# Layer 1's 3x3 convolutions in groups of four columns from six terms, and attention's order taken from a table

## The chip, the cores and the metric

The kernel runs on one core of one Trainium2 chip. The metric is device time in microseconds of one execution. Before the change it is 1324.69 us, the median of three runs (1323.67 to 1330.67). The profile comes from one more execution of its own.

## What is computed

The input x is 16 images of 128 channels and 32x32 pixels, all in float32. Two "metaformer" layers are applied, each with a mixer and a feed-forward part and with residual additions:

```
# layer 0
x = x + attention(ln_c(x))              # linear attention, 4 heads
t = tokens(x)                           # 1024 tokens x 128 channels for each image
t = t + stu(ln_t(t))                    # spectral convolution over the tokens + 3 taps
# layer 1
x = x + conv_block(ln_c(x))             # two 3x3 convolutions
t = tokens(x)
t = t + experts(ln_t(t))                # 64 experts, each takes its 8 best tokens
```

The convolution block is what the change rewrites first:

```
out = relu(bn(conv3x3(x, w1), gamma1, beta1, mean1, var1))
out = bn(conv3x3(out, w2), gamma2, beta2, mean2, var2)
return relu(out + x)                    # x is the normalized image here
```

## The kernel before, in words

The program runs stage after stage: **attention** (with the forward transform and the three taps of layer 0's feed-forward part) for 16 samples, **generation** (the spectral product, 16 chunks), **layer 1** for 16 samples (inverse transform, convolutions, routing, gates, pooling), the **experts** (16 groups of four, whose weights stream from memory), and a **final** addition and store. Inside a stage the samples overlap, and each engine works through its instructions in the order in which the program lists them (`tc.manual_schedule` pins PE, DVE, ACT and POOL). So the order of the list decides who waits for whom.

*Attention.* Class `Attention` has one method for each step of a sample. The order is a hand-written tuple `period` of 61 entries (name, distance): a loop over p from -6 to 15 runs each entry for sample p + distance, so seven samples are in flight and one sample is finished in each round. Work for later stages is cut in pieces and run between the entries: `filters()` builds the spectra of the filters and the mixed matrices `mst` (its 16 pieces `mi` are loaded and added on DVE, L662 to L667), and `prepare()` on POOL turns the 3x3 weights into the terms `cwd` (L678 to L694) and scales the inverse transform (L699 to L706). One piece of each runs in a round.

*Layer 1.* Class `Routed` has one method for each step of a sample. The order comes from `table`: each row has a name, an engine, a duration, a due time, the steps that it waits for and the buffers that it opens and closes. `planned()` (L1475) is a list scheduler that runs when the program is built: it takes, among the steps that can start within 0.25 us of the earliest one, the one with the smallest due time (offset + b x 54.66), with 0.15 us for a hop from engine to engine. A buffer that opens takes the slot that is free first.

*The convolutions.* A row of 32 columns is cut into 16 pairs. Two output columns come from four terms: the input terms are d0-d2, d1+d2, d2-d1 and d1-d3 of four neighbouring columns (`terms`, L914, on DVE, one instruction of 544 elements per partition for each term, from the padded planes `pads`); each term is multiplied by its own weights and summed over the three rows dy on PE (`products`, L922); and the two columns come back from sums and differences. An image is done in two halves of 16 rows. For one half of one convolution:

- `middle` (PE): terms 1 and 2, 2 x 3 products of 256 columns (L926) into one PSUM bank `pcv`, of which there are three;
- `shift` (ACT, L1097) copies one product out of PSUM; `sums` (DVE, L1105 and L1106) makes sum and difference;
- `outer` (PE): terms 0 and 3, again 2 x 3 products (L926);
- `rows` (DVE, L1115 and L1116) adds them; `relu` (ACT, L1119) writes the first convolution's result into the padded planes; `rows2` adds the residual (L1143) and the sample itself (L1145).

So one sample has 2 convolutions x 2 halves x 12 = 48 products of 256 columns. In the trace each float32 product is two records (2 x 16 x 48 = 1536). The other PE steps of a sample are `inverse` (L1039), transposes (L149, L159), `logits` (L1187), `turn` (L149) and `pool` (L1242); the last three run once for two samples. Of the buffers, the term tile `v` and the result tile `r` have two slots each, the PSUM tile `big` two, the token tile `tok` one.

*Loads.* SP issues nearly all transfers in its own queue. Layer 1 first loads `wi`, `cw`, the gate weights and `b1` (L890 to L901), then for each sample x and y (L942, L945). The experts' weights go through a ring of nine 1 MB slots (`RING`) made of tiles that layer 1 no longer needs: five slots are loaded after the last sample's `inverse`, four after its last `rows2`.

Of the kernel before, what the change touches and what calls it, by code (L numbers as in the profile page):

```python
# [1 line left out]

# [12 lines left out]
P = 128  # L15
# [15 lines left out]
NQ = 8  # L31
# [26 lines left out]
HP = H + 2  # L58
WP = W // 2 + 1
HR = H // 2  # L60
WT = W // 2
# [5 lines left out]
def metaformer_kernel(ctx: ExitStack, tc: tile.TileContext, io: dict, out: bass.AP):  # L67
# [96 lines left out]
    with ExitStack() as l0:  # L164
# [7 lines left out]
        cwd = [dram.tile([P, 3, 4, C], F32, name=f"cwd{n}", tag=f"cwd{n}") for n in range(2)]  # L172
# [32 lines left out]
        ph = lconst.tile([P, NCH, CW], F32, name="ph")  # L205


        with ExitStack() as a0:
# [96 lines left out]
            for b in range(2):  # L305
                load(b)
            wqk = aconst.tile([P, 2 * C], F32, name="wqk")
# [16 lines left out]
            nc.vector.tensor_scalar(mu[:, 0], mu[:, 0], wmix[:, 0:1], None, ALU.mult)  # L324
            for i in range(1, NF):
                nc.vector.scalar_tensor_tensor(
                    mu[:, i], mu[:, i], wmix[:, i : i + 1], mu[:, i - 1], ALU.mult, ALU.add
                )

# [11 lines left out]
            class Attention:  # L341
# [10 lines left out]
                def tokens(self):  # L352
                    if self.b + 2 < B:
                        load(self.b + 2)
# [37 lines left out]
                def norm(self):  # L392
                    normalize(self.tok, self.tok, self.sts[:, 0], self.sts[:, 3])
# [19 lines left out]
                def q_(self):  # L413
# [17 lines left out]
                def k(self):  # L431
# [69 lines left out]
                def fold2(self):  # L501
# [4 lines left out]
                def fold2_copy(self):  # L506
                    self.wt = work.tile([P, P], F32, name="wt", tag="wt")
                    nc.vector.tensor_copy(self.wt, self.pw)
# [37 lines left out]
                def norm2(self):  # L546
                    normalize(self.ub, self.ub, self.sts2[:, 0], self.sts2[:, 3])
# [64 lines left out]
                def taps(self):  # L612

                    self.pa = big()
                    for si, (lo, hi) in enumerate(SEGS):
                        for tap in range(KU):
                            a = max(lo, tap)
                            nc.tensor.matmul(  # L618
                                self.pa[:, a:hi], mu[:, NF - 1 - si, tap, :],
                                self.u[:, a - tap : hi - tap],  # L620
                                start=(tap == 0), stop=(tap == KU - 1),
                            )
# [5 lines left out]
            def filters():  # L628

                wfm = setup.tile([P, NQ // 2, 2 * P], F32, name="wfm", tag="mi")  # L630
# [970 lines left out]
```

## Time and profile before

| what | value |
|---|---|
| median of three runs | 1324.69 us |
| the profiled execution's own time | 1324.0 us |
| its span, first to last instruction | 1322.2 us |
| around the span | 1.8 us |
| mean granted TensorE clock | 0.971 |
| attention, 0 to 395 us | PE busy 54.65 of the first 80 us, 304.72 of the other 315 |
| generation, 395 to 681 us | PE busy 278.42 of 286 |
| layer 1 starts, 681 to 724 us | PE busy 19.81 of 43 |
| layer 1, 724 to 1182 us | PE busy 456.24 of 458 |
| its last serial chain, 1182 to 1217 us | PE busy 22.81 of 35 |
| experts, 1217 to 1290 us | DMA share 0.93 |
| final, 1290 to 1322 us | DMA share 0.64 |

The stage borders were read from the timeline; they are where the first or last instruction of a kind stands. "PE" is the matmul part of TensorE and "PEld" its weight load, which overlaps it. A busy PE says that matmuls were in flight, not that they ran at peak. In a group of instructions the "busy" figure is the union of their times, so that two instructions that overlap count once; the "mean" is that of one record from its start to its end, and for pipelined matmuls it is longer than the distance from one to the next. The chain of waits lists what ended last, step by step, and there the distance can be read.

### The profile page before, as it was taken

Reading aid. Unit: us, or ns where it says so; the run is one execution under the profiler, and the core shown is the slowest. Engines: PE = TensorE matmul, PEld = TensorE weight load, DVE = VectorE, ACT = ScalarE, POOL = GpSimd, SP = SyncE. Lnnn points to the kernel's source line nnn. Section 1 sums busy time; section 2 is a strip of 40 time slices with the busy share of each in tenths; the row PEclk is TensorE's granted clock in tenths of the full one; section 3 lists DMA queues with packets and bytes.
Section 4 is the critical chain, followed back from the end, with each engine's and each line's share of the span. In section 5 each row is a group of like instructions: output and inputs, shape, how many; then the busy total and the mean of one; then the engine's idle time right before and its main releaser. Section 6 shows DMA issues by size and latency. Waiting matters only on the chain. (4 is left out here: it accounts for less than half of the span.)

```text
span 1322.2 us, 33734 instructions
## 1 busy us (share of the span) xinstructions
PE 1216.7 (92%) x14116; PEld 990.8 (75%) x14116; DVE 907.2 (69%) x1982; ACT 705.2 (53%) x1424; POOL 503.3 (38%) x816
## 2 busy tenths in 40 slices
PE   4889999999998999999956999999999999996886
PEld 3777777777767888888846987989888888883443
DVE  5688887877765666776637767777778676772224
ACT  3777777777545666666623435545555454544111
POOL 2324545454685777777743111222212121110002
PEclk8899999999998999999987999999999999997998
DMA  7014343433344333333367211313122113007986
GB/s 268 17 35 140 118 134 112 144 124 121 114 149 145 127 125 127 127 121 119 107 235 182 70 48 49 88 27 111 32 80 64 33 49 127 17 24 260 374 329 255
DMA packets 87401, 162.99 MB, mean 123 GB/s; under 512 B 5584, under 2 KB 40784, under 8 KB 86864
## 3 DMA queue, kind: packets, MB, share of 16 engines
q1 hardware_dynamic: 86608, 158.33, 36.2%
q8 instruction: 111, 1.82, 0.6%
q0 software_dynamic: 640, 2.49, 0.5%
q14 instruction: 42, 0.34, 0.1%
HBM read 104.18 MB, written 56.62 MB: 122 GB/s over the span
## 5 line engine op out<-in xcount | busy, mean ns | idle before, releaser
L926 PE MATMUL pcv<-v,cw 128*128 128x256 f32 x1536 | 342.9, 380 | 0.0
L926 PEld LDWEIGHTS pcv<-v,cw 128*128 128x128 f32 x1536 | 286.8, 190 | 42.2 <-issue 5.7
L785 ACT COPY g<-pg 128x512 f32<-128x512 f32 x288 | 153.1, 591 | 102.8 <-PE pg L776 102.8
L783 DVE COPY g<-pg 128x512 f32<-128x512 f32 x224 | 145.8, 687 | 90.1 <-PE pg L776 90.1
L776 PE MATMUL pg<-ph,mst 32*128 32x128 f32 x4096 | 155.3, 287 | 4.5 <-ACT g L785 3.0
L776 PEld LDWEIGHTS pg<-ph,mst 32*128 32x128 f32 x4096 | 130.7, 190 | 30.8 <-issue 25.9
L796 PE MATMUL py<-g,v 128*32 128x128 f32 x4096 | 140.1, 276 | 3.8 <-POOL v L768 1.2
L796 PEld LDWEIGHTS py<-g,v 128*32 128x32 f32 x4096 | 105.3, 110 | 20.7 <-issue 2.4
L767 POOL TENSOR_TENSOR v<-xc 128x256 f32<-128x256 f32 x128 | 91.6, 741 | 71.6 <-PE py L796 62.5
L141 ACT ACTIVATE tok<-tok,sts 128x128 f32<-128x128 f32 x256 | 101.8, 481 | 23.8 <-POOL sts L1001 20.4
L132 DVE BATCH_NORM_STATS2 bst<-big 128x6 f32<-128x256 f32 x256 | 91.1, 417 | 19.5 <-PE big L154 12.1
L1066 POOL TENSOR_SCALAR sts<-bst 128x8 f32<-128x8 f32 x16 | 6.5, 406 | 235.7 <-DVE bst L132 235.7
L920 DVE TENSOR_TENSOR v<-pads 128x544 f32<-128x544 f32 x128 | 85.0, 723 | 9.9 <-ACT pads L1119 9.5
L618 PE MATMUL big<-u,mu 128*128 128x128 f32 (+4 forms) x384 | 86.0, 380 | 0.0
L274 POOL TENSOR_TENSOR xf<-ab 128x256 f32<-128x256 f32 x34 | 24.8, 730 | 132.0 <-DVE ab L241 131.9
L618 PEld LDWEIGHTS big<-u,mu 128*128 128x128 f32 x384 | 56.7, 191 | 18.0 <-issue 15.4
L1097 ACT ACTIVATE ct<-pcv,bn 128x256 f32<-128x256 f32 x64 | 30.3, 474 | 68.8 <-PE pcv L926 67.9
L551 PE MATMUL big<-wf,ub 128*128 128x256 f32 x256 | 62.0, 385 | 0.2
L149 PEld LDWEIGHTS big<-ident,x 128*128 128x128 f32 x384 | 47.3, 148 | 19.2 <-issue 7.2
L149 PE MATMUL big<-ident,x 128*128 128x128 f32 x384 | 53.6, 286 | 8.5 <-DVE x L1048 3.4
L1115 DVE TENSOR_TENSOR r<-pcv,cs 128x256 f32<-128x256 f32 x64 | 26.9, 420 | 49.0 <-PE pcv L926 48.2
L141 ACT ACTIVATE tt<-tt,sts 128x128 f32<-128x128 f32 x128 | 51.1, 480 | 9.2 <-POOL sts L1001 8.9
(231 smaller groups left out, 2271.3 us busy)
## 6 DMA issues: line engine op xcount, KB each, us to landing
we<-in_weight SPq DMA_DIRECT2D x32, 1024.0 KB, 9.7
vd<-xf SPq DMA_DIRECT2D x16, 1024.0 KB, 5.1
xc<-vd SPq DMA_DIRECT2D x64, 256.0 KB, 3.5
yd<-ys SPq DMA_DIRECT2D x32, 512.0 KB, 3.8
y<-yd SPq DMA_DIRECT2D x15, 896.0 KB, 6.5
x<-in_x SPq DMA_DIRECT2D x16, 512.0 KB, 4.1
mi<-in_M_phi SPq DMA_DIRECT2D x16, 512.0 KB, 4.9
xd<-x SPq DMA_DIRECT2D x16, 512.0 KB, 6.0
```

What stands on the lines that cost most here:

```text
L132: nc.vector.bn_stats(bst[:, j : j + 2, :].rearrange("p j s -> p (j s)"), src[:, j : j + 2, :].rearrange("p j c -> p c j"),)
L141: nc.scalar.activation(dst[:, j, :], src[:, j, :], AF.Identity, bias=nm[:, j : j + 1], scale=r[:, j : j + 1],)
L149: nc.tensor.transpose(pt[:, j, :], src[:, j * P : (j + 1) * P], ident)
L551: nc.tensor.matmul(dst, self.ub[:, q, :], wf[:, q, :], start=True, stop=True)
L618: nc.tensor.matmul(self.pa[:, a:hi], mu[:, NF - 1 - si, tap, :], self.u[:, a - tap : hi - tap], start=(tap == 0), stop=(tap == KU - 1),)
L767: nc.gpsimd.tensor_tensor(vv[:, x, 1:, bs], e, o, op)
L776: nc.tensor.matmul(pg[r][:, i], mst[rs, 4 * q + i, :], ph[rs, c, :], start=True, stop=True,)
L783: nc.vector.tensor_copy(dst, src)
L785: nc.scalar.copy(dst, src)
L796: nc.tensor.matmul(py[rows, x, kl, :], v[:, (x * NM + m) * JL + jl, 1 - ri : 3 - ri, :] .rearrange("p k b -> p (k b)"), g[:, ((x * 2 + ri) ...
L920: nc.vector.tensor_tensor(v[:, k], d[i], d[j], op)
L926: nc.tensor.matmul(pc[:, i], wt[:, dy, k, :], v[:, k, hf * HR + dy : hf * HR + dy + HR], start=(dy == 0), stop=(dy == 2),)
```

## The change

Three parts, in one diff.

**1. Four columns from six terms.** A row is cut into 8 groups of four columns. Four output columns come from six terms, so one convolution of a whole image is 6 x 3 products of 8 x 32 = 256 columns; the upper and lower rows are no longer padded, and the products of dy = 0 and 2 leave one row out (248 columns). The halves are gone: a product fills a bank for the whole image.

```
-        def products(v, wt, hf, ks):
-            pc = ps.tile([P, 2, HR, WT], F32, name="pcv", tag="cv", bufs=3)
+        def products(v, wt, ks):
+            pc = ps.tile([P, 2, IMG], F32, name="pcv", tag="cv", bufs=3)
             for i, k in enumerate(ks):
-                for dy in range(3):
+                for dy in (1, 0, 2):
+                    lo, hi = max(0, 1 - dy), min(H, H + 1 - dy)
                     nc.tensor.matmul(
-                        pc[:, i], wt[:, dy, k, :], v[:, k, hf * HR + dy : hf * HR + dy + HR],
-                        start=(dy == 0), stop=(dy == 2),
+                        pc[:, i, lo * GT : hi * GT], wt[:, dy, k, :],
+                        v[:, k, lo + dy - 1 : hi + dy - 1],
+                        start=(dy == 1), stop=(dy == 2),
                     )
```

The first convolution's terms are no longer made on DVE: PE multiplies the normalized tokens by a constant matrix `bt` (a new input), 8 products of 192 columns, and ACT copies them out of PSUM. The image itself is still transposed and copied, for the residual.

```
+            def terms(self, i):
+                pv = self.pv[i] = big().rearrange("p (j w) -> p j w", j=4)
+                for j in range(4):
+                    nc.tensor.matmul(
+                        pv[:, j, : NTERM * 4 * GT], self.tok[:, 4 * i + j], bt, start=True, stop=True
+                    )
+            def terms_copy(self, i):
+                rows = slice(i * H // 2, (i + 1) * H // 2)
+                nc.scalar.copy(
+                    va[:, :, rows].rearrange("p t (j r) g -> p t j (r g)", j=4),
+                    self.pv[i][:, :, : NTERM * 4 * GT].rearrange("p j (t w) -> p t j w", t=NTERM),
+                )
```

The second convolution's terms are made on DVE, from padded planes of 32 x 9 = 288 elements; two planes at once are 576 elements (`columns(i, k)` addresses column sets i and k).

```
+            def inside_terms(self):
+                v = self.v = vb
+                zt = self.zt = work.tile([P, 4, PLANE], F32, name="zt", tag="zt", bufs=1)
+                nc.vector.scalar_tensor_tensor(
+                    zt[:, 0:2], columns(2, 1), -4.0, columns(4, 3), ALU.mult, ALU.add
+                )
+                nc.vector.tensor_tensor(v[:, 1], zt[:, 0], zt[:, 1], ALU.add)
+                nc.vector.tensor_tensor(v[:, 2], zt[:, 0], zt[:, 1], ALU.subtract)
+            def next_terms(self):
+                v, zt = self.v, self.zt
+                nc.vector.tensor_tensor(zt[:, 2:4], columns(4, 3), columns(2, 1), ALU.subtract)
+                for k, f in ((3, 2.0), (4, -2.0)):
+                    nc.vector.scalar_tensor_tensor(
+                        v[:, k], zt[:, 3], f, zt[:, 2], ALU.mult, ALU.add
+                    )
+            def outer_terms(self):
+                v05 = self.v[:, 0::5]
+                nc.vector.scalar_tensor_tensor(
+                    v05, columns(0, 1), 4.0, columns(4, 5), ALU.mult, ALU.add
+                )
+                nc.vector.scalar_tensor_tensor(v05, columns(2, 3), -5.0, v05, ALU.mult, ALU.add)
```

The output columns come from three pairs of products, `inside` (terms 1, 2), `next` (3, 4) and `outer` (0, 5). ACT copies the second product of the first two pairs (256 elements each); the rest is on DVE. The shift of the first batch normalization moves into the relu's bias, that of the second into `rest`.

```
+            def inside_sums(self):
+                sd = self.sd = work.tile([P, 2, IMG], F32, name="cs", tag="cs")
+                m = self.pc[1, 2][:, 0]
+                nc.vector.tensor_tensor(sd[:, 0], m, self.cti, ALU.add)
+                nc.vector.tensor_tensor(sd[:, 1], m, self.cti, ALU.subtract)
+            def columns(self):
+                nd = work.tile([P, 2, IMG], F32, name="zt", tag="zt", bufs=1)
+                m = self.pc[3, 4][:, 0]
+                nc.vector.scalar_tensor_tensor(nd[:, 0], self.ctn, 0.5, m, ALU.mult, ALU.add)
+                nc.vector.scalar_tensor_tensor(nd[:, 1], m, 2.0, self.ctn, ALU.mult, ALU.subtract)
+                r = self.r = work.tile([P, 4, IMG], F32, name="r", tag="r", bufs=1)
+                nc.vector.tensor_tensor(r[:, 0:2], nd, self.sd, ALU.add)
+                nc.vector.scalar_tensor_tensor(r[:, 2:4], nd, 4.0, self.sd, ALU.mult, ALU.add)
+            def edges(self):
+                y03 = self.r[:, 0::3]
+                nc.vector.tensor_tensor(y03, self.pc[0, 5], y03, ALU.add)
...
+            def rest(self):
+                self.edges()
+                r = self.r
                 nc.vector.scalar_tensor_tensor(
+                    r, r, bn[:, 1, 1:2], self.p1.rearrange("p o h k -> p o (h k)"), ALU.add, ALU.add
+                )
+                xs = self.x.rearrange("p (n o) -> p n o", o=4)
+                nc.vector.scalar_tensor_tensor(
+                    xs, r.rearrange("p o n -> p n o"), 0.0, xs, ALU.max, ALU.add
                 )
```

The tiles `va` (first convolution), `vb` (second), `r` and `zt` have one slot each, `zt` now being shared by the inverse transform's odd classes, `columns` and the second convolution's terms. The weights grow from 4 to 6 terms (`cwd`, two loads of 1152 KB in place of 768 KB), and `prepare()` needs more steps on POOL for them: after the three scalings, 3 additions of 384 elements, a scaling of 768, then scaling, addition, scaling, 2 additions, a scaling of 768 and one more scaling, in place of 3 additions and a scaling of 768.

**2. Layer 1's table** is rewritten for these steps, with new due times (offset + b x 206.95). `planned()` gets `in_turn=True` here: a buffer takes its slots in rotation. `even` and `odd` are now one after the other, and samples may start at 0, 4, 8 and 12 us of the plan.

**3. Attention's order** comes from `planned()` as well. The tuple `period` is replaced by a table of the same steps with durations, due times (offset + b x 113.05) and buffers; `norm`, `norm2` and `taps` are cut in two. The filters are steps of the table (`f_mixes`, `f_negate`, `f_even` and so on). The pieces of `mst` may start at 30 + 10 b us and those of `prepare`, three at a time, at 70 + 17 b us of the plan. At the start x0, x1, `wf`, `phi` and x2 to x7 are loaded in this order, before the first 3x3 weights.

```
-                for p in range(-reach, B):
-                    next(preparing, None)
-                    for name, d in period:
-                        b = p + d
...
+            def ready(b, name):
+                if name == "tokens":
+                    return 2.0 * b if b < 2 else 8.5 + 1.5 * b
+                if name == "f_matrix":
+                    return 30.0 + 10.0 * b
+                if name == "prepare":
+                    return 70.0 + 17.0 * b
+                return inputs.get(name, 0.0)
+            inputs = dict(f_mixes=6.5, f_negate=6.0, f_even=9.5, f_odd=9.5)
...
+                for b, name in planned(
+                    table, buffers, B, 113.05, left_out, ready
+                ):
```

Around them: `b1` is loaded into `tok`'s slot after the last `image`; the ring's order is y, z, wi, y, cw0, v, cw1, zt, pad, with four slots loaded after the last `inverse`, one after the last `outer_a`, four after the last `rest`; the experts' outputs `ot` lie in `lg`'s slot and the gates of pair 4 in `tok`'s; the final stage's copy `yt` takes the slots of the weights.

## The prediction

> **What bounds the kernel now.** I read the busy shares first, then busy time by stage, then the chain of waits inside layer 1, then the rows of the instructions that go. The shares and the chain by line, from the page:
>
> ```profile
> PE 1216.7 (92%) x14116; PEld 990.8 (75%) x14116; DVE 907.2 (69%) x1982; ACT 705.2 (53%) x1424; POOL 503.3 (38%) x816
> ...
> PE pcv L926 25%; PE big L1039 4%; PE big L149 3%; PE big L159 2%; PE big L1187 1%; PE pp L1242 1%; PE peo L1405 1%; DMA we<-in_weight 1%; PE ph L1381 1%; PE pfy L1461 1%; PE ph L1374 1%; DVE ht L1396 1%; DMA y<-yd 1%; PE pht L1394 1%; DMA yd<-ys 0%
> ```
>
> PE is the busy one, and the products of the convolutions (L926) hold a quarter of the path. Shares are averages, so the same by stage (length; then busy time of PE, weight load, DVE, ACT, POOL; clock; DMA):
>
> ```profile
> 0.00:80.00 80.00, 54.65 (x282) 44.62 (x283) 51.45 (x176) 46.78 (x98) 20.95 (x33) 0.89 0.32 118
> 80.00:395.00 315.00, 304.72 (x1771) 237.22 (x1769) 246.98 (x564) 214.92 (x442) 164.19 (x265) 1.00 0.40 125
> ...
> 724.00:1182.00 458.00, 456.24 (x2693) 400.21 (x2692) 345.45 (x745) 230.20 (x464) 89.56 (x222) 1.00 0.20 59
> ...
> 900.00:1021.30 121.30, 121.30 (x740) 106.67 (x738) 94.91 (x206) 63.62 (x129) 25.77 (x64) 1.00 0.22 61
> ```
>
> In layer 1 PE never rests; DVE is idle over a fifth of the time. 121.30 us are four samples (the pooling, L1242, returns each 60.67 us for two), so a sample takes 30.33 us, with 23.7 of DVE and 15.9 of ACT. Attention is nearly as full after 80 us; its first 80 us leave PE 25 us idle. The chain of waits inside layer 1 gives distances, cleaner than means:
>
> ```profile
> 904.36 1.90 PE pp L1242 x32
> ...
> 920.48 10.36 PE pcv L926 x48
> ...
> 949.36 3.57 PE big L1039 x32
> ...
> 960.70 0.87 PE big L159 x8
> ```
>
> 48 records are 24 products: 0.432 us for 256 columns. Twice 10.36 is a sample's 48 products, 20.72 of its 30.33 us.
>
> **Part 1, PE in layer 1.** Removed: 20.72 us a sample. Added: 36 products, 12 of 256 columns (0.432) and 24 of 248 (0.418 by columns): 5.18 + 10.04 = 15.2. Also added: 8 products of 192 columns, 8 x 0.324 = 2.6, by columns from the same row. Net -2.9 us a sample, -46.6 for sixteen, all on the path while PE sets the pace. By columns is safe down to 128: L1039's sixteen products of 128 take 3.57 us, 0.223 each. If the 192-column products went at the weight load's mean of 190 ns a record, they would cost 3.0: 7 us in all, kept for the range.
>
> **Part 1, DVE.** The rows that go:
>
> ```profile
> L920 DVE TENSOR_TENSOR v<-pads 128x544 f32<-128x544 f32 x128 | 85.0, 723 | 9.9 <-ACT pads L1119 9.5 <-ACT pads L1083 0.4
> ...
> L1115 DVE TENSOR_TENSOR r<-pcv,cs 128x256 f32<-128x256 f32 x64 | 26.9, 420 | 49.0 <-PE pcv L926 48.2
> ...
> L1097 ACT ACTIVATE ct<-pcv,bn 128x256 f32<-128x256 f32 x64 | 30.3, 474 | 68.8 <-PE pcv L926 67.9
> ```
>
> Busy by count: a term 85.0 / 128 = 0.664; 256 elements 0.42; 512 elements (L1143) 0.69; 1024 (L1048) 1.22. Removed a sample: 8 terms 5.3, 16 instructions of 256 (sums and rows) 6.6, L1143 and L1145 twice 2.8: 14.7. Added, scaled between these rows (288: 0.45, 576: 0.70): inside sums 4 x 0.42 = 1.7; `columns` twice (2 x 0.42 + 2 x 0.69) = 4.4; edges 2 x 0.69 = 1.4; second terms 4 x 0.70 + 4 x 0.45 = 4.6; `rest` 2 x 1.22 = 2.4: 14.5. So DVE stays at 23.5 us, but of a 27.4 us sample: 86% in place of 78%. ACT: four shifts (1.9) go, four copies of 256 (0.386, L822: 1.5) and two of 768 (0.8, between L785's 0.59 for 512 and L1063's 1.01 for 1024) come: 15.9 + 1.2 = 17.1 us, 63%. Both remain beside PE's work; the cover is thinner.
>
> **What is late next.** The tile `r` has one slot, and its round for a sample is: columns 2.2, edges 0.7, two relus 1.25 (L1119), inside terms 1.6, two PE groups 5.1, copy 0.4, columns 2.2, rest 3.1, and eight hops of about 0.1: 17.4 us. It fits in 27.4, but 9.9 of it are DVE's, and DVE has 13.6 us of other work to place. Where an instruction of DVE stands in front, the products behind it wait on PE, and PE's queue with them. Two gaps in PE's chain can open: outer_a to inside_b (edges, relus, inside terms, hops: 3.9 us) and after outer_b (`rest` 3.1 us until the next columns may start). Each must be covered by PE's other 12.2 us a sample (inverse, transposes, terms, routing). Bounds: 0 idle (now 1.8 us of 458) to 7.0 a sample. I take 0.6, nearer to today's rows, since the same kind of order holds PE at 99.6% now and DVE still has 4 us a sample free: +10 us. The drain: nothing else covers the last sample's 3.9 us gap, and `rest` (3.1) ends later than the old last half (0.8 + 1.4): +3, bounds 0 to 5. Layer 1: -46.6 + 10 + 3 = **-34**.
>
> **Part 1, the borders of the stage.** Layer 1 starts after yd has been written (6.60 us) and y(1) read (9.03 us, until 702.4): the loads of weights grow by 0.86 MB with `bt` in front of them, issued when the last generation products free their memory at about 663; DMA's share from 660 to 680 is 0.52, so they hide there; uncovered they cost 2 us at the 410 GB/s seen at the start. `even` before `odd` puts 1.5 us of POOL ahead of DVE in the first sample, while `add` no longer stands behind y(1)'s landing (it waited from 701.4 to 705.6): 0, bounds -3 to +2. The ring still has five slots loaded before the last `rest` and four after it; the experts are DMA-bound (0.93) and stay. The gates of pair 4, on SP, now wait for `tok` until the last group has used `b1` and hold back pairs 5 and 6; they are needed last of eight: 0, bounds 0 to 2. `yt` in the weights' slots: 0.
>
> **Part 3, attention.** The taps are PE's last work for a sample, and their distance is the round (start, duration):
>
> ```profile
> 269.94 5.38 PE L618 MATMUL big<-u,mu 128*128 128x128 f32 x24
> ...
> 291.83 5.38 PE L618 MATMUL big<-u,mu 128*128 128x128 f32 x24
> ```
>
> 21.89 us, nine times over. Adding the starts of one round's PE groups where nothing waits gives 20.7; the rest is a wait for the normalized `ub` (L530) at `taps_in` and what follows it. An order that moves these apart can win 1.1; I take 0.6 in 11 rounds: -7. The fill: of 25 us idle in the first 80, 6 pass before the first product (6.18), and phi, behind the same loads as now, lands at 16.6. DVE and ACT are both under 65% there, so earlier samples can start earlier: -10. From 25 to 40 us the clock is at 0.50 to 0.58 with 10.5 us of matmuls; a fuller PE keeps some of the 5 us lost: -2. Attention: **-19**. Bounds: -36 (all of the 1.1 in 14 rounds, 15 of the idle, 5 of clock) to +8 (0.4 of new stalls in 20 rounds).
>
> The preparation adds to POOL, per convolution, from 5.2 us to 13.5 (five steps of 1.0, two scalings of 2.15, three more at half of 2.15), 17 us in all. Behind them on POOL stand `k_scale`, which PE's `context` waits for, and the butterflies. POOL is half idle there (164 of 315): 0; if each of some 16 pieces held PE up by half its 2.4 us, +19, a bound I keep only in part, as DVE's k_recip comes 2 us ahead of it. One row speaks against more POOL work: at 695.29 L966 on DVE takes 0.95 us beside a POOL addition and 0.42 at 702.87 without. [...]
>
> The sum against the profiled execution: 1324.0 - 34 - 19 = 1271, say **1270**. That execution stands 0.7 below the median, so nothing is to be added.
>
> **Rivals.**
> - *Attention's table wins nothing* (the round stays 21.9, the fill is bound by DVE's chain in each sample): 1324 - 34 = 1289. For it: PE is already 97% busy after 80 us.
> - *DVE at 86% shows on PE*: 1.5 us idle a sample, 1324 - 46.6 + 24 + 3 - 19 = 1285. For it: one slot each of `r`, `va`, `vb`, `zt`; against: DVE waits for PE today (L1115, 48 us).
> - *Better*: no new idle time in layer 1, attention near its bound: 1324 - 46.6 - 31 = 1246.
> - *It does not do what it says*: PE time does not follow columns (the 192-column products go at the weight load's 190 ns): 1277.
> - *Slower*: the two PE gaps between convolutions stay open because PE's order has nothing ready to put in. With 5 of the 7.0 us open: 1324 - 46.6 + 80 + 3 - 19 = 1341. It decides from 2.9 + (19 - 3) / 16 = 3.9 us a sample on. Against it: 12.2 us of other PE work a sample, and two samples' tiles alive.
>
> **How the numbers follow.** Chances: forecast 0.46, attention nothing 0.19, DVE 0.15, better 0.11, not by columns 0.03, slower 0.06. Low 1246 takes in the better case as far as its worked value, high 1308 the DVE rival with attention winning nothing (1304) and 4 us of the small bounds. About 0.5% is what a measurement can tell from no change. Faster by more 0.90, within 0.04, slower 0.06.
>
> **What would show it.** Layer 1: pooling every 54.8 to 57 us in place of 60.67, L926 at about 243 us in the chain's distances, PE idle near 10 us, DVE share about 0.85. Attention: taps about 21 us apart, the first of them well before 94.8, generation starting near 376 in place of 395. A PE gap after each `outer_a`, waiting for DVE terms, is the slower rival; waits of L618 or `context` on POOL are the preparation. I am wrong if the products do not shrink with columns, or if PE's idle time in layer 1 passes 3.9 us a sample.

## The result, and the profile after

The changed kernel takes 1331.65 us, the median of 20 runs, against 1324.87 us for 20 runs of the kernel before. The ratio is 1.0061, with a 95% interval of 1.0043 to 1.0079: **slower by 0.6%**. The forecast was 1270 us, faster.

First the shares, the chain that ended last by line, and the costliest group of PE, from the page of the changed kernel. A group's row ends with the idle time of its engine just before it and with what ended that:

```profile
PE 1187.6 (90%) x13988; PEld 962.0 (73%) x13988; DVE 954.5 (72%) x1918; ACT 725.1 (55%) x1456; POOL 509.4 (38%) x830
...
PE pcv L1058 18%; PE big L1222 3%; PE big L1172 2%; PE big L149 2%; PE big L159 2%; PE big L1396 1%; DVE bst L132 1%; DMA we<-in_weight 1%; PE peo L1620 1%; PE ph L1594 1%; PE ph L1587 1%; DVE v L1256 1%; DVE v L1253 1%; PE pfy L1676 1%; DVE ht L1611 1%
...
L1058 PE MATMUL pcv<-v,cw 128*128 128x248 f32 (+1 forms) x1152 | 262.5, 381 | 24.0 <-DVE v L1256 20.6
```

PE has 29 us less to do than before (1187.6 against 1216.7) and the span is 4.4 us longer. The products now stand behind 24.0 us of idle PE, nearly all of it ended by one DVE line, L1256, the second instruction of `outer_terms`; and two DVE lines that write the input terms (L1256 and L1253) have entered the chain. Next the stages of the changed kernel by windows (length; busy time of PE, weight load, DVE, ACT, POOL; clock; DMA):

```profile
0.00:80.00 80.00, 62.27 (x321) 49.03 (x322) 62.99 (x181) 51.13 (x106) 23.61 (x42) 0.89 0.38 139
80.00:395.00 315.00, 299.32 (x1726) 233.25 (x1725) 260.98 (x558) 212.96 (x434) 176.14 (x261) 0.99 0.38 120
...
725.10:1185.80 460.70, 433.94 (x2655) 380.41 (x2656) 377.90 (x712) 255.56 (x514) 83.78 (x236) 0.99 0.21 61
```

In attention PE did 7.6 us more by 80 us, and 5.4 us less in the 315 after it. In layer 1, from the first product of a convolution to the last, PE is idle for 26.8 us; in the kernel before it was 1.8 us of 463.5. Where the two spans differ, stage by stage, by the start and end of each stage's products in the two traces:

| stage | before, us | after, us | difference | forecast |
|---|---|---|---|---|
| attention, to the first generation product | 395.8 | 399.7 | +3.9 | -19 |
| generation | 273.2 | 273.3 | +0.1 | 0 |
| border, last generation product to first inverse product | 25.8 | 27.2 | +1.4 | 0 |
| layer 1, first inverse product to first expert product | 522.7 | 519.3 | -3.4 | -34 |
| experts and the end | 104.7 | 107.1 | +2.4 | 0 |

(A "generation product" here is one of L776, after the change L903, by its start; the spectral products that follow them, L796 and L923, lie in the border.)

Nearly all of the forecast's two gains is missing: of the 57 us between the sum of the forecast (1271) and the profiled execution (1328.4), layer 1 has 31 and attention 23. In layer 1 a pair of samples now takes 58.44 us by the starts of the logits (60.67 before, 56 forecast). What happens inside it is seen in the timeline of DVE and of PE in the changed kernel, in the middle of a sample (start, duration; the last bracket is the idle time before, and what ended it):

```profile
970.11 1.28 DVE L1245 TENSOR_TENSOR zt<-pads 128x576 f32<-128x576 f32 x1
971.42 1.24 DVE L1247 SCALAR_TENSOR_TENSOR v<-zt 128x288 f32<-128x288 f32 x2
973.15 0.76 DVE L1253 SCALAR_TENSOR_TENSOR v<-pads 128x576 f32<-128x576 f32 x1 [0.49 <-PE pcv L1058]
973.95 0.76 DVE L1256 SCALAR_TENSOR_TENSOR v<-pads,v 128x576 f32<-128x576 f32 x1
```

```profile
970.41 2.70 PE L1058 MATMUL pcv<-v,cw 128*128 128x256 f32 x12
974.76 2.60 PE L1058 MATMUL pcv<-v,cw 128*128 128x256 f32 x11 [1.64 <-DVE v L1256]
```

The group at 970.41 is `inside_b`, products of terms 1 and 2; the one at 974.76 is `next_b`, terms 3 and 4. Terms 3 and 4 were ready at 972.66, when L1247 ended. Yet `next_b` waits until L1256 is done, which writes terms 0 and 5; and L1253, the first to write those two, itself waits for `inside_b`, which reads neither. These two waits form a circle, and no data asks for them. The six terms lie side by side in one tile, and `outer_terms` writes slots 0 and 5 through one strided access, `v[:, 0::5]`, whose span covers slots 1 to 4. In one sample of a pair this leaves PE idle for 1.64 us, in the other for 0.49.

**Theories.** A: this wait, which comes from the span of one write, is what layer 1 loses. B, the rival that the forecast had named: DVE is the bound of layer 1 and the wait only shows it. For attention, C: GpSimd's preparation of the weights costs what the table gains; D: the table gains nothing by itself.

### The profile page after: what moved, and what is told of

The parts are those of the page before. It is cut to its first block, busy times and chain, and to the rows that moved or that the text cites. A ratio compares the mean times of both kernels' runs of the same rounds, so it can differ in the third digit from the quotient of the medians.

```text
span 1326.6 us, 33490 instructions
## 1 busy us (share of the span) xinstructions
PE 1187.6 (90%) x13988; PEld 962.0 (73%) x13988; DVE 954.5 (72%) x1918; ACT 725.1 (55%) x1456; POOL 509.4 (38%) x830
## 5 line engine op out<-in xcount | busy, mean ns | idle before, releaser
L1058 PE MATMUL pcv<-v,cw 128*128 128x248 f32 (+1 forms) x1152 | 262.5, 381 | 24.0 <-DVE v L1256 20.6
L1058 PEld LDWEIGHTS pcv<-v,cw 128*128 128x128 f32 x1152 | 215.0, 191 | 56.0 <-DVE v L1256 25.9
L903 PE MATMUL pg<-ph,mst 32*128 32x128 f32 x4096 | 152.7, 284 | 5.1 <-ACT g L912 3.7
L903 PEld LDWEIGHTS pg<-ph,mst 32*128 32x128 f32 x4096 | 128.3, 187 | 31.4 <-issue 26.0
L923 PE MATMUL py<-g,v 128*32 128x128 f32 x4096 | 141.1, 278 | 4.8 <-POOL v L895 2.0
L923 PEld LDWEIGHTS py<-g,v 128*32 128x32 f32 x4096 | 106.1, 110 | 21.9 <-POOL v L895 2.3
L132 DVE BATCH_NORM_STATS2 bst<-big 128x6 f32<-128x256 f32 x256 | 90.1, 416 | 25.2 <-ACT tt L1367 19.8
L474 POOL TENSOR_TENSOR ke<-ke,ks 128x1024 f32<-128x1024 f32 x16 | 32.6, 2035 | 102.4 <-DVE wt L521 35.0
L1266 ACT ACTIVATE ct<-pcv 128x256 f32<-128x256 f32 x64 | 24.2, 378 | 73.7 <-PE pcv L1058 73.7
L141 ACT ACTIVATE ub<-ub,sts 128x128 f32<-128x128 f32 x128 | 51.0, 480 | 21.6 <-DVE sts L557 21.5
L567 PEld LDWEIGHTS big<-wf,ub 128*128 128x128 f32 x256 | 47.1, 190 | 15.2 <-ACT u L592 3.7
```

The source lines that it names most:

```text
L132: nc.vector.bn_stats(bst[:, j : j + 2, :].rearrange("p j s -> p (j s)"), src[:, j : j + 2, :].rearrange("p j c -> p c j"),)
L141: nc.scalar.activation(dst[:, j, :], src[:, j, :], AF.Identity, bias=nm[:, j : j + 1], scale=r[:, j : j + 1],)
L567: nc.tensor.matmul(dst, self.ub[:, q, :], wf[:, q, :], start=True, stop=True)
L903: nc.tensor.matmul(pg[r][:, i], mst[rs, 4 * q + i, :], ph[rs, c, :], start=True, stop=True,)
L923: nc.tensor.matmul(py[rows, x, kl, :], v[:, (x * NM + m) * JL + jl, 1 - ri : 3 - ri, :] .rearrange("p k b -> p (k b)"), g[:, ((x * 2 + ri) ...
L1058: nc.tensor.matmul(pc[:, i, lo * GT : hi * GT], wt[:, dy, k, :], v[:, k, lo + dy - 1 : hi + dy - 1], start=(dy == 1), stop=(dy == 2),)
```

## The experiments

Each ratio is to the kernel before, run on the same chip beside it, with its 95% interval. Differences between two changed kernels are differences of these ratios, at 1324 us for 1.

### 1. The six terms in another order

```
-                v05 = self.v[:, 0::5]
+                v05 = self.v[:, 4:6]           # slots hold terms 1, 2, 3, 4, 0, 5
```

(the other writes of `v`, and the products of the second convolution, use the new slots)

> The changed kernel with its six terms of the second convolution stored in another order (1, 2, 3, 4, 0, 5), so that the last two terms (0 and 5) are written into two neighbouring slots instead of the first and the last of six. The computation is the same. Theory A (a wait that the code does not need): in the changed kernel the strided write of terms 0 and 5 spans the slots of terms 1 to 4, so it is ordered after the reads of terms 1 and 2, and the products of terms 3 and 4 wait for it: PE waited for L1256 20.6 us in 16 waits, 1.64 us idle in even samples and 0.49 in odd ones, about 17 us over the 16 samples. Theory A expects these waits gone, logits every 56 to 57 us per pair of samples instead of 58.44, and the whole 10 to 17 us shorter, 1315 to 1322 against 1331.65. Rival B (VectorE is the bound: 25.1 us busy of 29.2 a sample): the wait only moves to another VectorE step, logits stay at 58 or above, and the whole is 0 to 4 us shorter. [...]

Measured: **0.9856 (0.9822 to 0.9889)**, 27 us below the changed kernel. Logits come every 55.84 us, and layer 1 takes 494.2 us. The waits of PE in layer 1 (what waited, for what; us in total, times, longest), first in the changed kernel and then here:

```profile
PE pcv L1058 <- DVE v L1256: 20.6, 16, 2.3
PE pcv L1058 <- DVE v L1240: 3.1, 3, 2.2
```

```profile
PE big L159 <- ACT tt L141: 5.5, 1, 5.5
PE big L149 <- DVE x L1354: 3.2, 1, 3.2
PE pcv L1058 <- DVE v L1240: 3.2, 3, 2.2
```

The waits for L1256 are gone and none as large has come in their place. The same 260 us of the steady samples, changed kernel and this one:

```profile
845.00:1105.00 260.00, 249.35 (x1560) 218.78 (x1559) 223.72 (x423) 152.72 (x306) 53.54 (x144) 1.00 0.20 55
```

```profile
845.00:1105.00 260.00, 258.24 (x1644) 229.88 (x1643) 232.68 (x443) 155.04 (x317) 53.84 (x147) 1.00 0.23 69
```

DVE was busy for 223.72 us in the kernel where theory B has it as the bound, and does 232.68 us of work in the same time as soon as PE is let go: it was no bound, B is out. The gain is larger than the 10 to 17 us that theory A expected. In the two profiles layer 1 is 25.1 us shorter: the idle time of PE in it falls by 18.7 us (53.1 to 34.4), close to theory A's 17, and its busy time by 6.4 (466.2 to 459.8), for the same products, which theory A left out. By the logits, 13.0 us come from five steady pairs (2.6 each), 6.7 from the time until the first logits (102.0 to 95.3 us), where the same wait came up to 2.26 us long, and 5.3 from the last two pairs.

### 2 and 3. The last instruction of a sample, alone and with the slots

```
-                xs = self.x.rearrange("p (n o) -> p n o", o=4)
+                xs = self.x.rearrange("p (n o) -> p o n", o=4)
-                    xs, r.rearrange("p o n -> p n o"), 0.0, xs, ALU.max, ALU.add
+                    xs, r, 0.0, xs, ALU.max, ALU.add
```

> The changed kernel with one VectorE instruction, the last of a sample (L1354), walking its 1024 elements plane by plane: the columns are read in a row, and x with a stride of four, where it had been the other way round. The computation is the same. In the changed kernel the instruction takes 1965 ns, and L1350 of the same size 1280. If the order of the walk is what costs, it falls to about 1300 ns, 11 us less VectorE work over 16 samples; if any access with a stride of four costs the same, it stays near 1950. Theory A (the unneeded wait on terms 0 and 5 sets the pace): PE does not wait for this step in the steady stretch, so 0 to 4 us in time, the waits for L1256 stay near 20 us. Rival B (VectorE is the bound): logits every 57.1 us instead of 58.44, 9 to 11 us shorter in all.

Measured: 1.0057 (1.0037 to 1.0078), as the changed kernel. The rows of the last two DVE instructions of a sample (busy, mean ns), in the changed kernel and here:

```profile
L1354 DVE SCALAR_TENSOR_TENSOR x<-r,x 128x1024 f32<-128x1024 f32 x16 | 31.4, 1965 | 0.6
L1350 DVE SCALAR_TENSOR_TENSOR r<-r,bn,pads 128x1024 f32<-128x1024 f32 x16 | 20.6, 1284 | 0.6
```

```profile
L1354 DVE SCALAR_TENSOR_TENSOR x<-r,x 128x1024 f32<-128x1024 f32 x16 | 33.1, 2069 | 0.6
```

The changed kernel's walk is not quite what the expectation says: there `x` is read and written in a row and `r` is read in jumps of 256 elements. Here `r` is read in a row, and `x` is read and written at a stride of four. Both walks cost some 0.7 us more than L1350. So this edit took no work from DVE and says nothing between A and B.

> The two edits before this one together: neighbouring slots for terms 0 and 5, and L1354 walking plane by plane. Theory A: about what the slots give alone, plus at most 4 us: 12 to 20 us shorter than the changed kernel, 1312 to 1320, logits every 55.5 to 56.5 us, PE idle in the stretch of steady samples near 0.5 us a sample. Rival B (VectorE is the bound): the 11 us of L1354 and little more, 1318 to 1322. The end of layer 1 (from the sixth pair's logits to the last) stays near 105 us by both, since neither touches the order: if it does, what the steady stretch gains is all that is gained, and the kernel comes out 3 to 12 us below the kernel before.

Measured: 0.9878 (0.9843 to 0.9914), logits every 55.9 us, layer 1 in 494.9 us: what the slots give alone, within the interval. It is 24 us below the changed kernel, more than the 12 to 20 that A expected, as at experiment 1.

### 4 and 5. The attention, each way round

```
# 4: the changed kernel with the attention of the kernel before (period by hand, loads two ahead)
+            period = (("q_max", 3), ("out_add", 1), ("tokens", 6), ...
+                    next(preparing, None)
+                    next(preparing, None)      # two steps of the longer preparation
# 5: the kernel before with the attention's table, its loads and its prepare rows
```

> The changed kernel's layer 1 and weights (six terms), with the attention of the kernel before: its order written by hand as a period, the preparations taken two steps at a time in its rounds, loads two samples ahead. One part of the change undone. By the stages of the two profiles the table of the attention costs 4 us (first product of the generation at 399.74 against 395.76), so theory A (the table wins 7.6 us of PE in the fill and loses it and more in the steady rounds beside GpSimd) expects 1326 to 1329, the generation starting at 395 to 398. The rival, that the longer preparations (14 steps more of weights) cost what the table seems to cost, expects the generation at 399 or later here too and 1330 to 1333. If the forecast's gain of 19 us in attention were there and lost elsewhere, this kernel would be slower, 1345 or more.

Measured: 1.0012 (0.9988 to 1.0036), 6.5 us below the changed kernel; the generation starts at 391.8 us, sooner than either theory had it. No cost of the longer preparation shows in the order by hand: its rounds are 21.9 us, as before.

> The other part of the change alone: the kernel before (its four-term convolutions, weights and layer 1 unchanged) with the attention ordered by the changed kernel's table, the loads at its head as there, and the preparations in its slots, with the old, shorter preparation of the weights. The computation is the same. Theory A (the table loses in the rounds in which GpSimd prepares and VectorE's small steps stand beside it, and gains nothing at the end of the fill): generation starts at 396 to 400 against 395.76, and the whole is 0 to 5 us slower than the kernel before, 1320 to 1326 if that stands near 1321. The forecast's view, that the table is worth 19 us and that the longer preparation takes it back: generation at 376 to 385, 10 to 19 us faster than before.

Measured: **0.9989 (0.9966 to 1.0012)**, the generation at 397.5 us. With the old, short preparation the table is worth nothing that can be measured. D holds: the 19 us of the forecast are not there. The `taps_add` of the samples (the addition on DVE that ends a sample's attention) show where they go: the first starts at 107.5 us instead of 100.3 (+7.2), the ten gaps to the eleventh take 209.4 us instead of 218.0 (-8.6; the steady ones are 21.0 us against 21.9), and the last five take 79.2 instead of 76.1 (+3.1).

### 6, 9 and 12. The preparation of the weights on GpSimd

```
# 6: no arithmetic on raw and cw in prepare(); the DMAs and the yields stay
# 9: ready() for "prepare":
-                    return 70.0 + 17.0 * b
+                    return 200.0 + 10.0 * b
# 12: in place of each step of 1.0 us, and twice for each of 2.13 us:
+                            eng.memset(fill, 0.0)      # 1152 elements of the tile cw
```

> The kernel of e1_adjacent with GpSimd's preparation of the convolution weights left out (the raw weights are loaded and written as they are, with the same number of steps, so the convolutions compute with wrong weights); 34 us of GpSimd work go. All else in attention stays. Theory A (GpSimd's steps hold VectorE's small ones: 8 elements took 1.84 us beside a 1.91 us step of GpSimd against 0.16 alone): VectorE's busy time from 80 to 200 us falls from 110 by 6 us or more, the late rounds of 25.2 and 22.8 us come near 21, and generation starts 4 to 10 us sooner than in e1_adjacent (399.8), at 390 to 396. The rival, that the order of the table itself is what costs (few samples ahead at the end, 25.0 and 22.2 us between the last samples): generation stays at 397 to 401.

Measured: 0.9782 (0.9752 to 0.9812), 9.8 us below experiment 1, by the two intervals give or take 6; the generation at 390.0 us: 9.8 us too. The gaps between `taps_add` of 22.8 and 25.2 us became 19.9 and 24.1. The stretch from 80 to 200 us, in experiment 1 and here:

```profile
80.00:200.00 120.00, 107.42 (x598) 82.56 (x596) 109.06 (x222) 80.14 (x167) 68.17 (x94) 0.96 0.48 148
```

```profile
80.00:200.00 120.00, 112.12 (x670) 87.99 (x669) 110.71 (x250) 87.79 (x182) 51.40 (x83) 1.00 0.46 141
```

DVE's busy time did not fall as expected (110.7 against 109.1): it did more instructions in the same time, 250 for 222. C holds in its size, for the whole preparation: of its 34 us of GpSimd's work the kernel before has 16 too. A rival stands beside it, the granted clock: it was 0.96 in that stretch of experiment 1 and 1.00 here, and 0.04 of 120 us are near 5 us (an estimate from these two rows). Whether the preparation lowers the clock or the two merely fell together, no run separates.

> The kernel of e1_adjacent with GpSimd's preparation of the weights and of the inverse products started later in the attention's table: the first at 200 us and one more every 10 us in place of 70 and 17, until about 350. The computation is the same, and so is the rest of the order. e6_no_preparation, without the weights' part, began the generation at 390.0, and e1 at 399.8: 9.8 us. Theory A (GpSimd's steps cost where the table lets VectorE's small steps stand between full queues, from 80 to 200 us, where PE was busy 112.1 of 120 without them and 107.2 with them): the stretch from 80 to 200 becomes as in e6, PE 111 to 113, the cost behind 200 us is smaller, generation at 392 to 396. The rival, that a step of GpSimd costs the same wherever it stands: generation at 398 to 401, with rounds of 22 to 23 us from 200 to 330 in place of 21.2 to 21.9.

Measured: 0.9836 (0.9803 to 0.9869), 2.6 us below experiment 1 and within its interval; the generation at 397.6 us. Until 200 us it runs like experiment 6 (PE busy 111.9 of the 120 us), and then the gaps are 22.1 to 23.8 us where they had been 20.4 to 21.9. The rival fits better: steps that stand later lengthen the later rounds. That a step costs the same wherever it stands is not shown, since the 2.2 us between 397.6 and 399.8 are less than the spread given at experiment 12.

> The kernel of e1_adjacent with each step of the weights' preparation on GpSimd replaced by writing a constant into 1152 elements a partition (1.06 us for that size in L1036; two of them for each of the four steps of 2.13 us), at the same places: GpSimd stays as busy with it as before, 34 us, but reads nothing. The weights are written unprepared, so the convolutions compute with wrong weights; all else in attention stays. It separates two ways in which the 9.8 us between e1 (generation at 399.8) and e6 (390.0, no preparation) can come about. Theory A (a GpSimd step that reads holds up VectorE's steps with two inputs): the generation starts at 389 to 394 and the ratio to the kernel before is 0.976 to 0.981. The rival (GpSimd's queue: the scaling of the keys and the butterflies stand behind the preparation, and PE behind them): generation at 397 to 401, ratio 0.983 to 0.988.

Measured: 0.9845 (0.9810 to 0.9880), the generation at 394.8 us. The ratio is that of the rival, the start of the generation lies between both. This does not settle **how** the preparation costs its 10 us, by holding up DVE's steps or by standing in GpSimd's queue. The starts of the generation in single profiles are no finer: the same attention gave 395.7, 399.7, 399.8, 401.6 and 403.5 us in the five profiles that have it. The granted clock from 80 to 200 us goes with part of this: 0.99 in the first of these five, 0.96 or 0.97 in the others. The rounds are steadier. From the second `taps_add` to the eleventh these five take 190.4 to 195.1 us, this experiment 187.1 and experiment 6 187.0: in these rounds that speaks for reading as what costs, on one profile of each edit. The whole time does not show this gain.

### 7 and 8. Both repairs, and layer 1 in another order

> The neighbouring slots of e1_adjacent and the old attention of e4_old_attention together. If the two costs add (28 us from the slots, 6.5 from the attention, by the ratios 0.9856, 1.0012 and 1.0061 to the kernel before), the ratio is 0.981, 25 us below the kernel before, near 1296; if the attention's gain was chance between runs, it is as e1_adjacent, 0.985.

Measured: **0.9795 (0.9770 to 0.9820)**. The two costs add.

```
# 8: durations of the table as measured, due times and their spacing searched anew for them; for example
-            ("rest", "DVE", 3.4, 398.9, "columns_b outer_b", "", "cv:b05 r:b p1"),
+            ("rest", "DVE", 3.1155, 36633.82, "columns_b outer_b", "", "cv:b05 r:b p1"),
-        order = planned(table, buffers, B, 206.95, left_out, ready, True)
+        order = planned(table, buffers, B, 2831.5776, left_out, ready, True)
```

> As e7_adjacent_old_attention, with L1354 walking plane by plane as in e2_xorder, and with the due times of layer 1's table and their spacing found anew for the durations that the traces show (VectorE's steps of 256 elements 0.41 us, the last of a sample 1.28, and so on) in place of those in the table. A model of the queues with those durations gives 494 us for the changed kernel's order without the wait on terms 0 and 5 (494.2 measured in e1_adjacent from the first inverse product to the first expert product) and 479 for the new one. Theory (the end of layer 1 is a matter of the order): layer 1 takes 480 to 486, the last pair's logits follow the one before by under 40 us, the whole is 8 to 14 us below e7. The rival, that PE is full in layer 1 and only its work counts, gives 0 to 3 us.

Measured: 0.9845 (0.9819 to 0.9870), layer 1 in 495.7 us against 495.5 in experiment 7. The rival was right as to layer 1, and the model of the queues, which promised 15 us, was wrong. By the ratios the whole is 6.6 us slower than experiment 7; in the two profiles the difference lies in stages that the edit does not touch (the experts and the end took 111.7 us against 107.5), so it is not put down to the order. Two stretches of experiment 7 in the middle of layer 1 show why the new order gained nothing:

```profile
790.00:900.00 110.00, 109.12 (x698) 97.26 (x697) 98.44 (x186) 65.34 (x135) 23.99 (x64) 1.00 0.25 68
900.00:1010.00 110.00, 109.12 (x701) 98.21 (x701) 98.36 (x187) 65.45 (x133) 23.97 (x64) 1.00 0.26 68
```

With the wait gone PE is busy for 99.2% of the time: there is little left for an order to win there. At the end of the stage the new order won 2.7 us (from the sixth pair's logits to the first expert product, 118.1 us against 120.7), and it lost as much before that: pairs every 56.1 us against 55.9, the first logits 1.6 us later.

### 10. The loads of the weights behind the first loads of y

```
-        nc.sync.dma_start(bt, io["bt"])
-        for n in range(2):
-            nc.sync.dma_start(cw[n], cwd[n])
             for b in range(2):
                 load(b)
+            nc.sync.dma_start(bt, io["bt"])
+            for n in range(2):
+                nc.sync.dma_start(cw[n], cwd[n])
```

> The kernel of e7_adjacent_old_attention with the loads of the term matrix and of the two convolutions' weights (2.4 MB) issued behind the first two loads of y instead of ahead of the generation's end. The computation is the same. In e7 27.2 us lie between the last generation product and the first inverse one, 25.8 in the kernel before, whose weights are 0.86 MB less. If the larger loads take the writing and reading of y their share of DMA, the 27.2 falls to 25 or 26 and the first convolution product stands where it was or 1 us earlier: 1 to 2 us in all. The rival, that the weights then come late for the first convolution: its first product more than 25 us after the first inverse one, and 1 to 4 us slower.

Measured: **0.9767 (0.9734 to 0.9800)**, the fastest of all kernels here, some 31 us below the kernel before; its interval overlaps that of experiment 7. The border fell from 27.2 to 23.6 us. The chain of waits there, in the changed kernel and here (start, duration):

```profile
688.84 8.02 DMA yd<-ys
696.91 3.18 DMA y<-yd
```

```profile
677.14 3.60 DMA yd<-ys
...
680.79 3.22 DMA y<-yd
```

The last write of y took 6.60 us in the kernel before, 8.02 with the larger weights beside it, and 3.60 with none. PE waits for y for 14.8 us in experiment 7, as in the changed kernel, and 10.5 here. The first convolution product comes 25.6 us after the first inverse product, against 24.9 in experiment 7. The weights are not what it waits for: it starts at 709.86 us, and in the chain PE's own work stands ahead of it from 699.75 us on, with no load between.

### 11. Two writes in place of one strided one

```
-                v05 = self.v[:, 0::5]
-                nc.vector.scalar_tensor_tensor(v05, columns(0, 1), 4.0, columns(4, 5), ...)
-                nc.vector.scalar_tensor_tensor(v05, columns(2, 3), -5.0, v05, ...)
+                for i in range(2):             # term 0, then term 5
+                    vi = self.v[:, 5 * i]
+                    c = [columns(k, k + 1)[:, i] for k in (0, 2, 4)]
+                    nc.vector.scalar_tensor_tensor(vi, c[0], 4.0, c[2], ...)
+                    nc.vector.scalar_tensor_tensor(vi, c[1], -5.0, vi, ...)
```

> The changed kernel, slots as there, with each of the two instructions that write terms 0 and 5 replaced by two of half the size, one for each term, so that no write spans the slots between. The computation is the same; VectorE has four steps of 288 elements (0.46 us each) in place of two of 576 (0.76), 0.3 us a sample more. Theory A (the span of the strided write, not its layout or the order of the slots, made the wait): the waits for the terms of L1256 vanish as in e1_adjacent, logits every 55.8 to 56.3 us, layer 1 494 to 499 from the first inverse product to the first expert product, and the ratio to the kernel before 0.983 to 0.990. The rival, that the neighbouring slots helped in another way (a faster write or a faster read by the products): the waits stay near 20 us and the ratio is 1.00 to 1.01.

Measured: **0.9898 (0.9867 to 0.9929)**, logits every 56.3 us, layer 1 in 497.5 us. The slots are where the change put them, and DVE has more instructions. The longest waits of PE in layer 1 are now:

```profile
PE big L159 <- ACT tt L141: 5.8, 1, 5.8
PE big L149 <- DVE x L1354: 5.7, 7, 3.2
PE pcv L1058 <- DVE v L1240: 3.2, 3, 2.2
```

None for L1256. So it is the span of the write that made the wait, not its layout and not the order of the slots: A is shown by two different edits.

## Why the prediction was wrong, step by step

- **PE in layer 1: right.** Per sample it forecast 27.4 us of work and 28.0 us in time. Experiment 1 has 55.84 us a pair, 27.92 a sample, where PE's work can show: 12 records of products take 2.54 us in its chain of waits and a sample's terms 2 x 1.30, so 36 products come to 15.2 and the sample to 30.33 - 20.72 + 15.2 + 2.6 = 27.4. Products follow columns here: 1.69 ns a column in both rows (6 products of 1504 columns in all in 2.54 us, 4 of 192 each in 1.30).
- **What is late next: here it failed.** The step reads "I take 0.6, nearer to today's rows, since the same kind of order holds PE at 99.6% now". It looked for waits that the data make (`r`'s round, the gap from `outer_a` to `inside_b`, `rest`), and in the steady samples none of these opened. It did not ask what the new strided write `v[:, 0::5]` is ordered against. It named `va` and `vb` as tiles with one slot each, but not that six terms in one tile let a single write stand against the readers of four others. Experiments 1 and 11 take that wait away by two different edits, and PE's 20.6 us go. With the wait a sample takes 29.22 us, without it 27.92. In layer 1 the idle time of PE grew by 29.1 us (24.0 to 53.1), where 13 were forecast, and its busy time fell by 32.5, where 46.6 were. In experiment 1 the two are 10.4 and 38.9, in sum -28.5 against the -34 forecast.
- **DVE at 86%: wrong as a cause, right as a figure.** DVE's share in experiment 1 is 0.89 (232.68 / 260), and PE hardly waits for it (6.4 us in all). Its price per sample was 23.5 us and measured 25.1. Half of the difference is `rest`, taken at "2 x 1.22": its instructions take 1.28 and 1.97 us. The other half is the second terms, a mean of up to 1.05 us in the steady samples (L1245) where 0.70 was taken. The walk is what goes with the longer time in `rest`: 1.97 us with one operand read in jumps of 256 elements, 2.07 with one read and written at a stride of four (experiment 2), 1.28 with all in a row (L1350). In the kernel before, with two columns, `x` had a stride of two and paid nothing (L1145, 694 ns for 512 elements; L1143, 693). By what mechanism a walk costs this is not shown.
- **The slower rival: right sign, wrong mechanism.** It asked for 3.9 us of idle PE a sample, in the gap after `outer_a`, and 3.9 was also the forecast's sign of being wrong. The idle time grew by 1.8 us a sample only (29.1 / 16), and most of it (the 20.6 us) lay between `inside_b` and `next_b`. That was enough because attention gave nothing.
- **Attention: -19 forecast, nothing measured** (experiment 5, -1.5 us with an interval from -4.5 to +1.6). The rival "attention's table wins nothing" was right. Of its terms the steady rounds were right (-7 forecast, -8.6 in experiment 5). The fill was not: -10 forecast, +7.2 measured. In the changed kernel PE does 7.6 us more in the first 80 us, but on several samples at once; the first sample ends later, not sooner (its `taps_add` at 106.0 us against 100.3), and PE stands idle for 12.8 us from 80 to 200 us against 4.1 before. The 2 us from a higher clock, an estimate, did not come: with PE busy for 62.27 us against 54.65, the clock is 0.89 in the first 80 us of both. The end of the stage, which the forecast left out, gave back another 3.1.
- **The preparation: forecast 0 for the 17 us added; wrong in the table's order.** Experiment 6 measures 10 us for all 34 us of it. What the added part costs can be estimated from the ratios: six terms with their preparation add 1.0061 - 0.9989 in the table's order and 0.0012 in the order by hand, and the difference is 8 us, give or take 5. The step took 0, with the words "POOL is half idle there (164 of 315)". The sum of idle time was no cover in an order that leaves PE 0.3 us idle in 130 (129.7 of 130 from 200 us on): in experiment 9 steps put there lengthen the rounds. In the order by hand each round waits anyway, 21.9 us with the longer preparation or the shorter.
- **The borders: forecast 0 with bounds of -3 to +2, measured +1.4,** and experiment 10 points to the cause, the larger loads beside the last write of y (8.02 us against 6.60).
- **Two slips in the working** change no decision: 1324 - 34 is 1290, not 1289, and the preparation's "five steps of 1.0" are six additions, with which its 13.5 us come out.

What stays open is how GpSimd's steps cost. In the changed kernel a small step of DVE can be as long as the step of GpSimd beside it:

```profile
68.91 0.16 DVE L125 SCALAR_TENSOR_TENSOR ga<-ga 128x1 f32<-128x1 f32 x1
69.11 1.84 DVE L126 SCALAR_TENSOR_TENSOR ga<-ga 128x1 f32<-128x1 f32 x1
```

```profile
69.03 1.91 POOL L474 TENSOR_TENSOR ke<-ke,ks 128x1024 f32<-128x1024 f32 x1 [7.98 <-DVE ga L124]
```

Here 0.16 us becomes 1.84, for one element a partition (the expectation of experiment 6 calls it 8), and the instruction ends 0.01 us after GpSimd's addition. The table put such meetings into most samples (of the eleven L391 from 80 to 330 us six take 1.79 to 1.80 us, two 0.49 to 0.50 and three 0.16, a mean of 1110 ns, and 1049 without the preparation; the same step, L381 in the kernel before, takes 159 ns in the order by hand). If reading on GpSimd is what holds these steps up, writing a constant should have freed them. L385 does fall from 254 ns in experiment 1 to 186 in experiment 12, as without the preparation, and L391 stays at 1111. The rounds of experiment 12 speak for it (the 187.1 us above), but the whole gained nothing measurable over experiment 1: that this is where the 10 us go is not shown.

## What to carry to other kernels

When a step is rewritten to write several parts of a tile at once, list what else lives between the first and the last element of that write, and who reads it: a strided write can be ordered against all of it, and a wait between two steps that share no data, each way round, is its sign in the trace. A group's row names the line that ends a wait; whether the data ask for that wait is a question to the code. And idle time added up over a stage does not say that added work hides: here the order that packed PE to 99.8% paid for it, and in the one that waited in each round no price showed.

## What had not been expected of the hardware

A float32 instruction of DVE over 1024 elements took 1.97 us with one operand read in jumps of 256 elements, 2.07 with one read and written at a stride of four, and 1.28 with all in a row; 694 ns for 512 elements at a stride of two was no longer than without. An instruction of 128x1 elements took 1.84 us beside a 1.91 us step of GpSimd. Stages that no edit touches differ between profiles: the experts and the end took 104.7 to 112.2 us, so that whole kernels are compared here by ratios and not by single spans.
